# A message-passing network on one core: the edge weights leave the one-hot matrix, the features become three bf16 terms, and GpSimd multiplies

## The chip, the cores and the metric

The kernel runs on one core of a Trainium2 chip. Its time is device time in microseconds; the smaller is the better. TensorE is called PE, VectorE DVE, ScalarE ACT, GpSimd POOL and SyncE SP, as the profiles call them. PEld is PE's weight load.

## The reference

128 graphs of 64 nodes, 128 features a node, go through four layers, each a residual with a layer norm. The first two are continuous-filter layers on the dense matrix `adj` of distances; the last two are graph convolutions with a normalised adjacency. Cut to what the change touches:

```python
# layer 0 (20 Gaussians, cosine cutoff at 5)
y = x @ w_in2f
W = ssp(f_ij @ fw1 + fb1) @ fw2 + fb2          # a filter of 128 values for every pair (i, j)
W = W * rcut[..., None]
agg = jnp.einsum('bjf,bijf->bif', y, W)
x = _layernorm(x + ssp(agg @ ow1 + ob1) @ ow2 + ob2)

# layer 1 (64 Gaussians, the edge weight A is adj itself, and it enters twice)
Wf = Wf * Am
y = jnp.einsum('bjf,bijf->bif', rf, Wf * Am)

# layers 2 and 3: graph convolutions with d^-1/2 (A + I) d^-1/2
```

So each edge (i, j) takes the features of node j, times a filter that depends on its distance, times a weight (`rcut` in layer 0, the square of `adj` in layer 1), and sums over j.

## The kernel before

Only edges are computed. Two graphs (a pair) are worked on together, graph 0 on partitions 0 to 63 and graph 1 on 64 to 127 wherever a tile is laid out by node. A first part, `compact`, sorts each row's edges into fixed slots: nodes are ordered by degree, and each row of eight nodes gets a fixed number of slots (141 in layer 0, 162 in layer 1). Of each slot three numbers are written to DRAM: the distance `d`, the neighbour's index `j` (bf16), and the weight `w`. For 8 pairs (a set) this is one bundle; the compaction of sets 1 to 7 runs beside the main loop, seven steps (`run(early, 7)`) and one scatter step (`run(side, 1)`) per iteration. POOL issues its indirect scatters and packing copies.

The main loop has 2 x 64 pairs (64 of layer 0, then 64 of layer 1) and three chunks a pair, 384 chunks and as many iterations. A chunk is 2 x 376 slots in layer 0 and 2 x 432 in layer 1. Its steps:

- `loads(n)`: SP reads d, j and w of a pair from DRAM, the same row broadcast to many partitions; w goes to the 64 partitions of its graph.
- `gaussians`: ACT squares and exponentiates d, ahead of the pair.
- `filter_in` (px, L1466): PE's first filter layer; ACT turns it into h with Exp and Ln (L740, the line of the helper that records all ACT work).
- `one_hot` (hot, L1451): DVE makes the matrix that gathers, `(j == row) * w`, 128 partitions, fp32.
- `gather` (pg, L1492): two fp32 matmuls of 64 rows, features times that matrix; ACT copies the result to SBUF as `g`.
- `filter_out` (pw, L1479): PE's second filter layer, 128 rows, fp32.
- `message` (m, L1507): DVE, `(pw + b2) * g`, pw in PSUM and g in SBUF.
- `slot_sums` (agg, L1525): eight DVE reduces per pair, three per iteration.

Iteration i runs `filter_in` of chunk i, `gather` of chunk i-1, and `filter_out` and `message` of chunk i-2. Between these stand single steps of generators (queues `nodes`, `befores`, `convs`, `last`) that `slot` advances: `node_before` (features of the next group of four pairs: transpose xT, copy xt L1226, matmul y L1232), `node_after` (zero entries' share in layer 0, output layers, back permutation, layer norm L1200 to L1207), and `graph_convs` (layers 2 and 3 for a group). A step that ends with a matmul group is followed, at the next `slot`, by the step that reads it:

```python
        before, owing = owing, None
        held = run(queue, 1)
        if before is not None and before is not queue:
            run(before, 1)
```

All engines run their instructions in exactly this written order (`in_order` at the end makes it so), and the DMAs of SP stand in one queue. In the groups that matter four pairs make twelve chunks, and I write "a group" for that. `late_constants` makes the vectors dinv2 and dinv3 of the convolutions, with two powers on POOL (L1168, L1171), near pairs 52 to 56.

Of the kernel before, what the change touches and what calls it, by code (L numbers as in the profile page):

```python
# [11 lines left out]
F32 = mybir.dt.float32  # L12
# [565 lines left out]
def sparse_stack(ctx: ExitStack, tc: tile.TileContext, t: dict, out: bass.AP, flag):  # L578
# [9 lines left out]


    nc = tc.nc  # L590
    x, adj = t["x"], t["adj"]
# [172 lines left out]
    ident = const.tile([P, P], F32, name="ident")  # L764
    make_identity(nc, ident)
    ones = const.tile([3, P], BF16, name="ones")
    nc.vector.memset(ones, 1.0)
# [256 lines left out]
    def loads(n):  # L1024


        layer, p = divmod(n, NP)
        size = GSLOTS[layer]
        s, at = p // 8, (p % 8) * 2 * size
        assert (layer, s) in stored, "slots are read before they are written"  # L1030
        d = edge.tile([P, GSLOTS[1]], F32, tag="d", name=f"d_{n}", bufs=3)
        j = edge.tile([P, GSLOTS[1]], BF16, tag="j", name=f"j_{n}")
        w = edge.tile([P, GSLOTS[1]], F32, tag="w", name=f"w_{n}")

        def load(to, name, first, n):

            nc.sync.dma_start(to, dram_ap(slots[layer, name][s], first, [[0, to.shape[0]], [1, n]]))

        if layer == 0:
            third = 2 * size // 3  # L1040
            for q in range(3):
                load(d[32 * q : 32 * (q + 1), 0:third], "d", at + q * third, third)
            d = d[0:96, 0:third]
        for b in range(2):
            rows, first = slice(A * b, A * (b + 1)), at + b * size
            if layer == 1:
                load(d[rows, 0:size], "d", first, size)
            load(j[rows, 0:size], "j", first, size)
            load(w[rows, 0:size], "w", first, size)
        return d, j, w  # L1050

# [99 lines left out]
    def late_constants():  # L1151


        eye = const.tile([P, A], F32, name="eye")
        nc.vector.tensor_add(eye, ident[:, 0:A], ident[:, A : 2 * A])
        deg = const.tile([P, NP], F32, name="deg")
        for s in range(NS):
            part_ = a_all[:, part(s), 0:A]
            nc.vector.tensor_add(part_, part_, eye.unsqueeze(1).to_broadcast([P, 8, A]))
            nc.vector.tensor_reduce(deg[:, part(s)], part_, AX.X, ALU.add)  # L1160
            yield
        g["dinv2"] = const.tile([P, NP], F32, name="dinv2")
        g["dinv3"] = const.tile([P, NP], F32, name="dinv3")
        some = const.tile([P, NP], F32, name="some")

        nc.vector.tensor_scalar(some, deg, 0.0, None, ALU.is_gt)
        nc.vector.tensor_scalar(g["dinv2"], deg, TINY, None, ALU.max)
        nc.gpsimd.tensor_tensor(g["dinv2"], g["dinv2"], neg_half, ALU.pow)  # L1168
        nc.vector.tensor_mul(g["dinv2"], g["dinv2"], some)
        nc.vector.tensor_scalar(g["dinv3"], deg, GCN_EPS, None, ALU.add)  # L1170
        nc.gpsimd.tensor_tensor(g["dinv3"], g["dinv3"], neg_half, ALU.pow)  # L1171
        yield

# [15 lines left out]
    def once(name, n, q):  # L1189

        if n < GS and rings:
            return tiled(name, n, q)
        return node.tile([P, GS * P], F32, tag=name, name=f"{name}_{q}", bufs=1)[:, 0 : n * P]

# [20 lines left out]
    def node_before(layer, q):  # L1215
# [19 lines left out]
        yield True  # L1235
        y = node.tile([P, n, C], F32, tag=f"y{n}", name=f"ys_{name}", bufs={GS: 3, 2: 1, 1: 2}[n])
        act(y, ps, AF.Copy)
        feats[layer, q] = y
        yield

    zblk = const.tile([P, GS, P], F32, name="zblk")
    nc.gpsimd.memset(zblk, 0.0)

    def zero_share(q, agg):

        n = agg.shape[1]
        rows = zero_rows.pop(q)
        for b in range(2):
            at = slice(b * A, (b + 1) * A)
            nc.vector.tensor_scalar(zblk[at, :, at], rows[at], 0.0, None, ALU.is_equal)  # L1250
        yield
        _, ps = bank(f"zT_{q}", n)
        for s in range(n):
            nc.tensor.transpose(ps[:, s, :], zblk[:, s, :], ident)
        yield True
        zt = by_pair(once("zt", n, q))
        act(zt, ps, AF.Copy)
        yield
        _, ps = bank(f"zs_{q}", n)
        y = feats[0, q]  # L1260
        for s in range(n):
            nc.tensor.matmul(ps[:, s, :], lhsT=y[:, s, :], rhs=zt[:, s, :], start=True, stop=True)
        yield True
        nc.vector.scalar_tensor_tensor(agg, ps, zero_filter, agg, ALU.mult, ALU.add)
        yield

    def load_nodes(layer, q):
# [5 lines left out]
        if layer == 0:  # L1273
            rows = node.tile([P, GS, A], F32, tag="zr", name=f"zr_{q}")
            for s in range(GS):
# [170 lines left out]
    def one_hot(n):  # L1446

        _, j, wt = slot_data[n]
        size = GSLOTS[n // NP]
        hots[n] = edge.tile([P, GSLOTS[1]], F32, tag="hot", name=f"hot_{n}")  # L1450
        nc.vector.scalar_tensor_tensor(  # L1451
            hots[n][:, 0:size], j[:, 0:size], near, wt[:, 0:size], ALU.is_equal, ALU.mult
        )
# [30 lines left out]
    def gather(c):  # L1484
# [3 lines left out]
        at = slice(c["k"] * n, (c["k"] + 1) * n)  # L1488
        y = feats[c["at"]][:, c["s"], :]
        for b in range(2):  # L1490
            rows = slice(A * b, A * (b + 1))
            nc.tensor.matmul(  # L1492
                ps[:, b, 0:n], lhsT=y[rows, :], rhs=hots[c["n"]][rows, at],
                start=True, stop=True,
            )
        g_ = work.tile([P, 2, CHUNKS[1]], F32, tag="g", name=f"g_{c['id']}")
        c["g"] = g_[:, :, 0:n]
        act(c["g"], ps[:, :, 0:n], AF.Copy)

    def message(c):  # L1500
# [36 lines left out]
    last = []  # L1537
    slot_data, messages, aggs = {}, {}, {}

# [11 lines left out]
    for n in range(2):  # L1551
        slot_data[n] = loads(n)
    for s in (1, 2):
        load_set(s)
    run(deque([permuted(1), node_before(0, 0)]), -1)
    gaussians(0, 0)
    gaussians(0, 1)
    early = deque([gathering()])

# [21 lines left out]


    block = nc.cur_bb.bb.instructions
    before_loop = block[-1]
    past = [None] * 2
    for i in range(3 * N + 2):
        n, k = divmod(i, 3)
        c, c1, c2 = None, *past
        run(sums, 3)
        run(early, 7)  # L1590
        run(side, 1)
        if i == 3 * (NP + 1):
            assert not early and not side, "edges are still to be gathered"
            compacting.close()
# [7 lines left out]
        if n < N:  # L1602
# [6 lines left out]
            if k == 0:  # L1609
                if n + GS < N:  # L1610
                    ahead(n)
                if n + 2 < N:
                    slot_data[n + 2] = loads(n + 2)
                if c["s"] == min(2, len(range(NP)[GROUPS[layer][q]]) - 1):
                    load_nodes(layer, q)
                one_hot(n)
            filter_in(c)
        slot(nodes)
        if k < 2 and befores:
            slot(befores)  # L1620
# [7 lines left out]
        if k < 2 and n + 1 < N:  # L1628
            gaussians(n + 1, k)
        if c1 is not None:  # L1630
            gather(c1)
        slot(convs[1])
        for queue in last:
            slot(queue)
        past = [c, c1]
    run(sums, -1)
# [51 lines left out]
```

## Time and profile before

| | |
|---|---|
| median of 3 runs | 1931.93 us (1928.95 to 1933.0) |
| the profiled execution | 1935.16 us, span of its instructions 1933.4 us |
| mean granted TensorE clock | 0.950 |
| start, until the first chunk's Exp | 88.2 us |
| pairs 0 to 64 (layer 0) | 88.2 to 963.1 us |
| pairs 64 to 128 (layer 1) | 963.1 to 1855.7 us, last chunk's Exp |
| tail | 1855.7 to 1933.4 us |
| bytes moved by DMA | 214.96 MB, mean 111 GB/s |

The page gives busy time of each engine and its share of the span; a busy PE is not PE at its peak, since matmuls overlap. In a group's row the last part is: busy time of the group, mean duration of one instruction in ns, then idle time of the engine just before them and what ended it. An instruction's line is that of `kernel.py` before the change, and line numbers after it are larger by up to 25.

### The profile page before, as it was taken

The page shows a single profiled execution, that of the slowest core. Times are in us where ns is not written, and L with a number is a line of the kernel's source. Part 1 is how long each engine was busy: PE and PEld are TensorE (multiplying, and loading weights), DVE is VectorE, ACT ScalarE, POOL GpSimd, SP SyncE. Part 2 cuts the span into 40 slices and gives each one's busy share as a digit, 9 for nine tenths or more (in the row PEclk, how much of TensorE's full clock was granted, in tenths as well). Part 3 has the DMA queues.
Part 4 walks back from the last instruction along what each step waited for, and adds up shares of the span by engine and source line. Part 5 has one row for each costly group of instructions (what it writes and reads, how often), then busy time and mean ns, then how long its engine had stood idle before and what let it go on. Part 6 is the DMA issues. An engine that isn't in the chain of part 4 may idle for free.

```text
span 1933.4 us, 23695 instructions
## 1 busy us (share of the span) xinstructions
PE 1633.8 (85%) x6790; PEld 803.8 (42%) x6790; DVE 1587.6 (82%) x4298; ACT 1431.7 (74%) x1679; POOL 625.9 (32%) x920
## 2 busy tenths in 40 slices
PE   0288888788887999969988999999999999999975
PEld 0133343343333444424443544444454444444444
DVE  6579889888988777767778888888888888988984
ACT  1277767777766888848898978878888788888840
POOL 2423424342332232141112123323223333322435
PEclk9999898988998999979999999999999999999985
DMA  5355444363443444424566544645455455554400
GB/s 140 87 130 125 110 112 113 91 140 99 101 106 90 110 119 111 112 55 104 122 140 141 135 118 112 137 113 139 119 121 137 110 126 120 128 129 119 105 7 13
DMA packets 120595, 214.96 MB, mean 111 GB/s; under 512 B 41845, under 2 KB 68614, under 8 KB 120454
## 3 DMA queue, kind: packets, MB, share of 16 engines
q1 hardware_dynamic: 111776, 207.19, 44.4%
q0 software_dynamic: 4352, 5.02, 0.8%
q10 hardware_dynamic: 4326, 1.13, 0.3%
q8 instruction: 56, 0.92, 0.2%
q14 instruction: 85, 0.70, 0.1%
HBM read 200.92 MB, written 12.34 MB: 110 GB/s over the span
## 4 chain that ended last, share of the span: by engine, by line
PE 44%; DVE 33%; ACT 8%; issue 6%; POOL 3%; DMA 3%; SPq 1%; DVEq 0%; POOLq 0%; ACTq 0%
PE pw L1479 16%; DVE m L1507 9%; PE pg L1492 8%; DVE agg L1525 7%; PE px L1466 7%; DVE hot L1451 3%; ACT g L740 2%; PE y L1232 2%; ACT h L740 2%; ACT d L740 2%; PE back L1320 2%; DVE st L1200 2%; DVE mv L1201 2%; PE u L1291 1%; DVE at L961 1%
## 5 line engine op out<-in xcount | busy, mean ns | idle before, releaser
L740 ACT ACTIVATE g<-pg 128x752 f32<-128x752 f32 (+1 forms) x384 | 321.2, 836 | 255.8 <-PE pg L1492 249.2
L1525 DVE TENSOR_REDUCE agg<-m 128x16 f32<-128x336 f32 (+11 forms) x1024 | 417.1, 460 | 2.1
L740 ACT ACTIVATE h<-h,half 128x752 f32<-128x752 f32 (+2 forms) x385 | 372.4, 967 | 12.5
L1492 PE MATMUL pg<-hot,ys 64*128 64x376 f32 (+1 forms) x1536 | 374.3, 565 | 0.1
L1479 PE MATMUL pw<-h,w_L_gnn_fw 128*128 128x376 f32 x768 | 314.4, 536 | 35.8 <-DVE m L1507 35.7
L1507 DVE SCALAR_TENSOR_TENSOR m<-pw,c_L_gnn_b,g 128x432 f32<-128x432 f32 x384 | 245.1, 662 | 105.1 <-PE pw L1479 89.5
L1479 PE MATMUL pw<-h,w_L_gnn_W2T 128*128 128x432 f32 x768 | 321.2, 541 | 3.7 <-DVE m L1507 3.7
L1507 DVE SCALAR_TENSOR_TENSOR m<-pw,c_L_gnn_fb,g 128x376 f32<-128x376 f32 x384 | 219.7, 604 | 104.3 <-PE pw L1479 101.7
L1205 POOL TENSOR_TENSOR rs<-rs,neg_half 128x4 f32<-128x4 f32 (+2 forms) x70 | 68.6, 980 | 572.3 <-DVE rs L1203 570.4
L740 ACT ACTIVATE h<-px,c_L_gnn_b 128x864 f32<-128x864 f32 x192 | 187.4, 976 | 66.0 <-PE px L1466 66.0
L1479 PEld LDWEIGHTS pw<-h,w_L_gnn_fw 128*128 128x128 f32 x768 | 145.4, 209 | 150.6 <-DVE m L1507 66.0
L1492 PEld LDWEIGHTS pg<-hot,ys 64*128 64x128 f32 x1536 | 119.0, 190 | 202.1 <-ACT h L740 85.2
L1466 PE MATMUL px<-d,fw 32*128 32x376 f32 x768 | 180.4, 546 | 23.5 <-ACT h L740 21.1
L1479 PEld LDWEIGHTS pw<-h,w_L_gnn_W2T 128*128 128x128 f32 x768 | 131.9, 190 | 145.8 <-issue 90.4
L1451 DVE SCALAR_TENSOR_TENSOR hot<-j,row,w 128x1128 f32<-128x1128 bf16 (+1 forms) x128 | 191.3, 1495 | 0.0
L1466 PE MATMUL px<-d,w1t 64*128 64x432 f32 x768 | 178.4, 541 | 0.0
L740 ACT ACTIVATE h<-px,c_L_gnn_fb 128x752 f32<-128x752 f32 x192 | 169.6, 883 | 10.3 <-PE px L1466 6.2
L740 ACT ACTIVATE d<-d,neg_off 96x752 f32<-96x752 f32 (+1 forms) x128 | 145.0, 1133 | 0.0
L1466 PEld LDWEIGHTS px<-d,fw 32*128 32x128 f32 x768 | 59.7, 189 | 131.6 <-issue 66.0
L868 POOL DMA_INDIRECT rows<-comb,goes x64 | 70.6, 1103 | 121.9 <-DMA rows<-comb,goes 88.1
L1207 POOL TENSOR_SCALAR x_all<-ny,mv,rs 128x128 f32<-128x128 f32 x128 | 100.4, 795 | 3.6
L1466 PEld LDWEIGHTS px<-d,w1t 64*128 64x128 f32 x768 | 68.3, 186 | 56.2 <-issue 40.2
(210 smaller groups left out, 2078.6 us busy)
## 6 DMA issues: line engine op xcount, KB each, us to landing
d<-d_dram SPq DMA_DIRECT2D x128, 324.0 KB
w<-w_dram SPq DMA_DIRECT2D x128, 324.0 KB
w<-w_dram SPq DMA_DIRECT2D x128, 282.0 KB
j<-j_dram SPq DMA_DIRECT2D x128, 162.0 KB
j<-j_dram SPq DMA_DIRECT2D x128, 141.0 KB
d<-d_dram SPq DMA_DIRECT2D x192, 94.0 KB
x_all<-in_x_dram SPq DMA_DIRECT2D x8, 512.0 KB
cb<-code_dram SPq DMA_DIRECT2D x31, 128.0 KB
```

The costliest lines, as they stand in the source:

```text
L740: latest = nc.scalar.activation(out_, in_, func, **kw)
L868: nc.gpsimd.indirect_dma_start(out=into, out_offset=bass.IndirectOffsetOnAxis(ap=at, axis=0), in_=rows, in_offset=None,)
L1200: nc.vector.bn_stats(stats[:, s, :], y[:, s, :])
L1201: nc.vector.bn_aggr(mv[:, s, :], stats[:, s, :])
L1205: nc.gpsimd.tensor_tensor(rstd, rstd, neg_half[:, 0:n], ALU.pow)
L1207: nc.gpsimd.tensor_scalar(dst[:, s, :], y[:, s, :], mv[:, s, 0:1], rstd[:, s : s + 1], ALU.subtract, ALU.mult,)
L1451: nc.vector.scalar_tensor_tensor(hots[n][:, 0:size], j[:, 0:size], near, wt[:, 0:size], ALU.is_equal, ALU.mult)
L1466: nc.tensor.matmul(ps[:, b, 0:n], lhsT=w["w1"][rows, :], rhs=d[rows, col : col + n], start=True, stop=True,)
L1479: nc.tensor.matmul(ps[:, 0 : c["size"]], lhsT=c["w"]["w2"], rhs=c["h"][:, b, :], start=True, stop=True)
L1492: nc.tensor.matmul(ps[:, b, 0:n], lhsT=y[rows, :], rhs=hots[c["n"]][rows, at], start=True, stop=True,)
L1507: nc.vector.scalar_tensor_tensor(messages[n][:, b, at], c["pw"][b][:, 0:size], c["w"]["b2"], c["g"][:, b, :], ALU.add, ALU.mult,)
L1525: nc.vector.tensor_reduce(av[:, :, :, r], v[:, :, :, BASES[layer][r] : BASES[layer][r] + CAPS[layer][r]], AX.X, ALU.add,)
```

## The change

The one-hot matrix holds only zeros and ones, in bf16. The features are kept as three bf16 terms whose sum is the fp32 value, so that a gather is three bf16 products per graph, added up in PSUM. The weights are loaded on all 128 partitions, both graphs side by side, and POOL multiplies g by them in place after ACT's copy.

```diff
 node_before
-        y = node.tile([P, n, C], F32, tag=f"y{n}", ...)
-        act(y, ps, AF.Copy)
+        y = node.tile([P, 3, n, C], BF16, tag=f"y{n}", ...)
+        rest = by_pair(node.tile([P, 512], F32, tag="xt", ...)[:, 0 : n * P])
+        act(y[:, 0], ps, AF.Copy)
+        nc.vector.tensor_sub(rest, ps, y[:, 0])
+        nc.gpsimd.tensor_copy(y[:, 1], rest)
+        nc.gpsimd.tensor_tensor(y[:, 2], rest, y[:, 1], ALU.subtract)
 one_hot
-        hots[n] = edge.tile([P, GSLOTS[1]], F32, tag="hot", name=f"hot_{n}")
-        nc.vector.scalar_tensor_tensor(
-            hots[n][:, 0:size], j[:, 0:size], near, wt[:, 0:size], ALU.is_equal, ALU.mult
-        )
+        hots[n] = edge.tile([P, GSLOTS[1]], BF16, tag="hot", name=f"hot_{n}")
+        nc.vector.tensor_scalar(
+            hots[n][:, 0:size], slot_data[n][1][:, 0:size], near, None, ALU.is_equal
+        )
 gather
-        for b in range(2):
-            rows = slice(A * b, A * (b + 1))
-            nc.tensor.matmul(
-                ps[:, b, 0:n], lhsT=y[rows, :], rhs=hots[c["n"]][rows, at],
-                start=True, stop=True,
-            )
-        g_ = work.tile([P, 2, CHUNKS[1]], F32, tag="g", name=f"g_{c['id']}")
+        for i in range(3):
+            for b in range(2):
+                rows = slice(A * b, A * (b + 1))
+                nc.tensor.matmul(
+                    ps[:, b, 0:n], lhsT=y[rows, i, c["s"], :], rhs=hots[c["n"]][rows, at],
+                    start=i == 0, stop=i == 2,
+                )
+        g_ = work.tile([P, 2, CHUNKS[1]], F32, tag="g", name=f"g_{c['id']}", bufs=3)
         act(c["g"], ps[:, :, 0:n], AF.Copy)
+        nc.gpsimd.tensor_tensor(c["g"], c["g"], weights[c["n"]][:, :, at], ALU.mult)
 load_weights (new; the weights leave loads)
+        weights[n] = edge.tile([P, 2, GSLOTS[1]], F32, tag="w", name=f"w_{n}")
+        for b in range(2):
+            load_slots(weights[n][:, b, 0:size], "w", n, b * size)
```

The order changes with it. `gather` works on the chunk of its own iteration, no longer on the one before; `one_hot` of the next pair and `load_weights` two pairs ahead stand at the end of a pair's third iteration; a `befores` step runs in one iteration of three, no longer in two:

```diff
-        if k < 2 and befores:
+        if k == 1 and befores:
             slot(befores)
...
-        if c1 is not None:
-            gather(c1)
+        if c is not None:
+            gather(c)
+        if k == 2 and n + 1 < N:
+            one_hot(n + 1)
+        if k == 2 and n + 2 < N:
+            load_weights(n + 2)
...
-        if i == 3 * (NP + 1):
+        if i == 3 * (NP + 6):
             compacting.close()
```

In `late_constants` the two powers of 128x64 become sixteen of 128x8, seven early steps apart:

```diff
-        nc.gpsimd.tensor_tensor(g["dinv2"], g["dinv2"], neg_half, ALU.pow)
+        for i in (2, 3):
+            dinv = g[f"dinv{i}"]
+            for s in range(NS):
+                yield from (None for _ in range(7))
+                nc.gpsimd.tensor_tensor(dinv[:, part(s)], dinv[:, part(s)], neg_half[:, 0:8], ALU.pow)
```

The share of the zero entries in layer 0 (`zero_share`) goes the same way, a bf16 transpose and three bf16 products. Tiles `no` and `ny` share buffers with `na` and `nh`.

## The prediction

> **What bounds the kernel now.** I read the page first: who is busy, and the chain that ended last.
>
> ```profile
> PE 1633.8 (85%) x6790; PEld 803.8 (42%) x6790; DVE 1587.6 (82%) x4298; ACT 1431.7 (74%) x1679; POOL 625.9 (32%) x920
> PE 44%; DVE 33%; ACT 8%; issue 6%; POOL 3%; DMA 3%; SPq 1%; DVEq 0%; POOLq 0%; ACTq 0%
> PE pw L1479 16%; DVE m L1507 9%; PE pg L1492 8%; DVE agg L1525 7%; PE px L1466 7%; DVE hot L1451 3%; ACT g L740 2%; PE y L1232 2%; ACT h L740 2%; ACT d L740 2%; PE back L1320 2%; DVE st L1200 2%; DVE mv L1201 2%; PE u L1291 1%; DVE at L961 1%
> ```
>
> PE and DVE share the chain. The gather (pg, 8%) and the one-hot (hot, 3%) are what the change shrinks; POOL, where the new product goes, is two thirds idle. Next the windows, cut where the timeline shows the work to change: pairs 76 to 124 (steady layer 1), then pairs 40 to 52 and 52 to 56 of layer 0.
>
> ```profile
> 1114.00:1801.40 687.40, 644.54 (x2845) 326.33 (x2846) 600.34 (x1277) 571.28 (x627) 227.71 (x256) 1.00 0.52 124
> 655.00:798.50 143.50, 132.52 (x561) 62.52 (x560) 108.29 (x232) 119.23 (x152) 42.49 (x64) 0.98 0.45 115
> 798.50:868.00 69.50, 48.93 (x190) 22.89 (x190) 47.35 (x102) 40.22 (x51) 29.35 (x18) 0.83 0.30 74
> ```
>
> After length come PE, PEld, DVE, ACT and POOL busy, granted clock, DMA share, GB/s. I reckon per group: four pairs, twelve chunks. Steady layer 1 is 12 groups of 57.3 us: PE 53.7 busy, DVE 50.0, ACT 47.6, POOL 19.0. PE is within 3.6 us of the whole. The third row is one group that took 69.5 us where its neighbours take 47 to 48. The same query at every 100 us gives for 100 to 600 us (layer 0 beside compaction, groups of 57.7 us) DVE 88.3%, PE 84.0%, POOL 35.0%: there DVE is the fuller. Last, the groups by form, the waits, and single instructions in the timeline:
>
> ```profile
> L1492 PE MATMUL pg<-hot,ys 64*128 64x432 f32 x768 | 191.1, 575 | 0.1
> L1492 PE MATMUL pg<-hot,ys 64*128 64x376 f32 x768 | 183.1, 555 | 0.1
> L1451 DVE SCALAR_TENSOR_TENSOR hot<-j,row,w 128x1296 f32<-128x1296 bf16 x64 | 99.8, 1560 | 0.0
> L1451 DVE SCALAR_TENSOR_TENSOR hot<-j,row,w 128x1128 f32<-128x1128 bf16 x64 | 91.5, 1430 | 0.0
> ```
>
> ```profile
> PE y L1232 <- DVE xt L1226: 48.3, 21, 4.5
> ```
>
> ```profile
> 305.05 1.61 DVE L911 TENSOR_SCALAR w<-dc 128x141 f32<-128x141 f32 x1
> ...
> 486.44 2.17 DVE L1451 SCALAR_TENSOR_TENSOR hot<-j,row,w 128x1128 f32<-128x1128 bf16 x1
> ...
> 842.12 10.58 POOL L1168 TENSOR_TENSOR dinv<-dinv,neg_half 128x64 f32<-128x64 f32 x1 [34.38 <-DVE dinv L1167]
> ...
> 854.03 2.88 PE L1479 MATMUL pw<-h,w_L_gnn_fw 128*128 128x376 f32 x4 [12.11 <-DVE m L1507]
> ...
> 1232.61 1.27 POOL L1394 TENSOR_TENSOR x_all<-x_all,b_L_gnn_b 128x512 f32<-128x512 f32 x1
> ...
> 1748.31 0.73 POOL L1228 TENSOR_TENSOR x_all<-x_all,b_L_gnn_bd 128x256 f32<-128x256 f32 x1
> ```
>
> Three things to see. POOL's two-input product is straight in its size: 0.73 us for 256 elements, 1.27 for 512. One long POOL instruction (the power, 10.6 us, twice) stopped DVE and then PE for 12 us. And DVE and POOL block each other: the one-hot of 486.44 usually takes 1.38 us, but began under a POOL product (486.14 to 487.41) and took 2.17; POOL products that begin under a one-hot take 2.3 to 2.5 us instead of 1.27. The L911 row takes 0.24 us elsewhere and here waited behind four POOL instructions in a row.
>
> **The change, part by part.** *Gather.* A chunk's two fp32 products are issued as four matmuls (1536 in 384 chunks); busy time per chunk is 183.1/192 = 0.95 us (layer 0) and 191.1/192 = 1.00 (layer 1). K=128 of the same width takes 321.2/192 = 1.67 us, so the two 64-row halves overlap. No bf16 matmul of this shape is in the trace; the nearest (bias row, 3x512, L1422) is one instruction where fp32 needs two. I count an fp32 matmul as twice two passes: eight passes become six, at equal overlap three quarters: -0.24 and -0.25 us per chunk, about -94 us of PE in all. Bounds: perfect overlap of three pairs, a bf16 pass at half an fp32 instruction's serial share (1.67/8 = 0.21 us), 0.63 us per chunk (-143); per instruction, not per pass, 6 x 0.25 = 1.5 us (+190). I stay at three quarters because the time of px, 32 rows a tile, also goes by overlap, not count.
>
> *One-hot.* 128 times 1.43 or 1.56 us becomes a one-input compare, bf16 to bf16. Nearest: DVE's bf16 add, 682 ns for 1024 and 1213 for 2048, 0.52 ns an element plus 0.15 us: 0.73 and 0.82 us; not below half of that, not above today's. -92 us of DVE. [...]
>
> *Weights by POOL.* 192 products of 752 and 192 of 864 elements. From the two rows above, 2.1 ns an element plus 0.18 us: 1.78 and 2.02 us, 730 us on POOL. The third term and the copy (L1253 of the new file, a cast and a subtract of 512) are about 0.7 + 1.27 us per group; DVE gets one subtract of 512, 0.68 us. POOL per layer-1 group: 19.0 + 12 x 2.02 + 2.0 = 45.2 of 57.3. What hides it: the gather now runs an iteration earlier, so a product has more than one iteration (4.8 us) between ACT's copy and the message. Without that cover every chunk pays its 2 us. Queued behind a waiting product on POOL are the layer norms (4.2 us), conv scalings and scatters. They need at most 2 us of DVE's lead, so I cost no stall there.
>
> *The port.* This is the term without a price. A DVE operation that met a running POOL product waited out its rest less 0.15 to 0.2 us. Message and reduce, DVE's bulk, read one operand from SBUF and show no lengthening (604 against 604 ns under POOL work). Exposed per layer-1 group: four one-hots, a node add (L1307), two ELU adds (L1344), one compare (L1304), 8; in the compacting stretch about 15. POOL products run 40 to 45% of the time, mean rest 1 us: 0.35 us each from products, up to 0.55 with other POOL work in layer 1. Ends: 0, and 1.4 us (the L911 row less its usual 0.24). I take 0.55 x 8 = 4.5 and 0.35 x 15 = 5.2 us per group. [...]
>
> *Moved.* befores step at k = 1 only: PE's y matmuls come three iterations after the copy they waited for, 48.3/21 = 2.3 us each, mostly layer 0. The power becomes 16 short ones (rows of 1, 2, 4 columns: 0.57, 0.72, 1.03 us, so about 1.65 at 8), one per iteration. SP: the weights double (282 KB to 564, 324 to 648 KB, 256 times); in layer 1 +0.66 MB per 14.3 us on 124 GB/s lifts the share from 0.52 to about 0.71. SP now waits for POOL's last product of a pair before loading weights, and d and j of a later pair stand behind that; they have a pair's time, 14 us, and the present bursts last about 7 us, so nothing is charged. Later closing of the compaction pool, shared tags and bf16 zero share: under 3 us, nothing.
>
> **The sum.** Layer 1, 12 groups: PE 53.7 - 3.0 = 50.7; DVE 50.0 - 3.0 + 0.7 + 4.5 = 52.2; POOL 45.2. With the 3.6 us that lie beside the fullest engine now, 54.3 by PE, 55.8 by DVE; I take 55.5: -22 us. Compacting, 9 groups: DVE 50.9 - 2.8 + 0.7 + 5.2 = 54.0, but its 6.8 us idle shrinks by PE's 2.9 and the y wait's 2.3: about -0.5 each, -5. Pairs 40 to 52, three groups, DVE light: -3.5 each (the gather and half the y wait), -10. Group 52 to 56: 69.5 back to its neighbours' 48, less about 5 for a crowded POOL: -18. Pairs 56 to 76: five groups at -2.5, -12. Tail -2, first weights +3. Sum -66. The profiled execution took 1935.2 us (span 1933.4, 1.8 around it), so 1869; its median run is 1931.9, 3 us less: 1866.
>
> **The rivals.** *One, slower:* the port. If an exposed DVE operation waits 0.9 us (POOL fuller, its instructions back to back as before the L911 row), layer-1 DVE is 54.9 and the group about 58.3 (+12 us), the compacting group 62.3 busy and 64.5 long (+61), pairs 40 to 76 keep -5, the power -18: +50, about 1982. It decides from about 0.6 us a wait. For it: POOL goes from 35% to about 75% busy there. Against: waits outside products are rare. The variant with instructions priced alike in the gather ends there too. *Two, faster:* the compare is twice as fast, the port waits are under 0.2 us, PE sets the pace: layer 1 -36, compacting 9 x -5 = -45, the rest -50: 1801. For it: message and reduce never slowed. *Three, loads:* the wait on SP makes d late by half a microsecond per pair, 128 x 0.5 = +64: 1930, no change. That the change does not do what it says is not open: the new order holds 384 POOL products and six gather matmuls a chunk.
>
> **How the numbers follow.** Forecast (1830 to 1905) 0.45, rival two 0.22, rival three 0.10, rival one 0.23. Differences under 0.2% (4 us) cannot be told here. Rival three splits 0.04 faster, 0.04 same, 0.02 slower: faster 0.71, same 0.04, slower 0.25. The range 1790 to 1980 leaves out the far half of rival one and the tip of rival two.
>
> **What would show it.** Gather busy per chunk near 0.72 us; hot 0.5 to 0.85 us with some at 2; POOL product rows near 1.8 and 2.0 us; no 12 us PE gap; y waits gone; DVE m waiting for POOL g seldom. A large "DVE m <- POOL g" or hot rows of 2 us and more throughout prove rival one; ACT waiting for DMA d proves rival three.

## The result and the profile after

The changed kernel takes 2021.68 us (median, 2017.44 to 2026.69), the kernel before beside it 1932.47 us (1928.95 to 1934.61): a ratio of 1.0465, 95% interval 1.0436 to 1.0493. It is slower by 89 us where I forecast 66 us less. Its profiled execution took 2017.44 us, with a span of 2015.6.

The page of the changed kernel, busy time and the chain that ended last:

```profile
PE 1612.4 (80%) x7622; PEld 786.2 (39%) x7622; DVE 1649.2 (82%) x4333; ACT 1433.5 (71%) x1679; POOL 1386.3 (69%) x1386
DVE 27%; PE 24%; POOL 20%; issue 11%; DMA 10%; ACT 5%; SPq 1%; POOLq 0%; DVEq 0%; ACTq 0%
PE pw L1498 10%; POOL g L1519 8%; DVE m L1528 6%; DVE agg L1546 6%; DMA d<-d_dram 4%; DMA rows<-comb,goes 4%; POOL x_all L1219 3%; PE px L1485 3%; PE pg L1512 3%; DVE hot L1470 3%; POOL perm L871 2%; ACT g L741 2%; POOL rows L871 2%; DVE er L1364 2%; PE u L1311 1%
```

Of the four compute engines only POOL is fuller than before by share (32% to 69%), and it is still not full; PE and ACT fell, DVE stayed at 82%. What the chain shows is hand-over: POOL went from 3% to 20%, DMA from 3 to 10, PE from 44 to 24. Time is lost between engines, not on one of them. The windows of steady layer 1 (pairs 76 to 124, 12 groups of four pairs), of the compacting stretch (pairs 4 to 40, 9 groups) and of the group 52 to 56:

```profile
1143.80:1875.90 732.10, 643.27 (x3130) 328.82 (x3130) 637.74 (x1291) 571.28 (x625) 524.62 (x424) 0.96 0.57 160
139.00:687.70 548.70, 422.73 (x1927) 190.96 (x1928) 459.15 (x1624) 381.94 (x471) 383.92 (x488) 0.85 0.48 141
838.70:897.30 58.60, 49.22 (x217) 22.50 (x218) 47.03 (x102) 40.22 (x51) 35.82 (x35) 0.80 0.41 127
```

A layer-1 group takes 61.0 us (57.3 before), a compacting group 61.0 (57.7). In layer 1 PE is busy 53.6 us per group, as before (53.7), though its gather became lighter; DVE has 53.1, POOL 43.7. The fullest engine now leaves 7.4 us of a group idle, where it left 3.6. The clock in layer 1 fell from 1.00 to 0.96. Group 52 to 56, where the long powers stood, came down from 69.5 to 58.6.

The groups of instructions, by form:

```profile
L1519 POOL TENSOR_TENSOR g<-g,w 128x864 f32<-128x864 f32 x192 | 390.7, 2039 | 195.8 <-ACT g L741 175.0 <-issue 19.4 <-POOL blocks L1380 0.7
L1519 POOL TENSOR_TENSOR g<-g,w 128x752 f32<-128x752 f32 x192 | 343.0, 1789 | 156.6 <-ACT g L741 153.1 <-DMA zr<-perm 1.7
L1512 PE MATMUL pg<-hot,ys 64*128 64x376 bf16 x1152 | 139.5, 352 | 6.9 <-DVE hot L1470 6.4 <-ACT g L741 0.5
L1512 PE MATMUL pg<-hot,ys 64*128 64x432 bf16 x1152 | 139.1, 347 | 14.3 <-ACT g L741 9.8 <-DVE hot L1470 4.4
L1470 DVE TENSOR_SCALAR hot<-j,row 128x1296 bf16<-128x1296 bf16 x64 | 67.4, 1053 | 0.0
L1364 DVE SCALAR_TENSOR_TENSOR er<-em,er 128x512 f32<-128x512 f32 x30 | 52.6, 1755 | 0.0
L1215 DVE TENSOR_SCALAR rs<-mv 128x4 f32<-128x4 f32 x61 | 24.8, 407 | 2.1
```

The gather has 278.6 us, 95.6 less. The one-hot of 1296 columns takes 0.54 us when nothing hinders it (its lowest records), but 1.05 on average. The ELU add (er) took 681 ns before and takes 1755; the layer norm's add of four columns (rs) went from 169 to 407, and single ones to 1.85 us. The waits:

```profile
PEld pw L1498 <- DVE m L1528: 156.9, 194, 6.8
DVE m L1528 <- POOL g L1519: 71.5, 45, 6.8
ACT d L741 <- DMA d<-d_dram: 48.8, 27, 4.6
```

PE's weight loads wait twice as long for the message as before (156.9 us for 80.3), the message waits for the product, and ACT waits for distances, which it did not before. One case from the timeline of the changed kernel (start, length):

```profile
1407.70 1.25 PE L1498 MATMUL pw<-h,w_L_gnn_W2T 128*128 128x432 f32 x3
...
1412.06 2.01 POOL L1519 TENSOR_TENSOR g<-g,w 128x864 f32<-128x864 f32 x1 [2.40 <-ACT g L741]
1412.24 1.85 DVE L1215 TENSOR_SCALAR rs<-mv 128x4 f32<-128x4 f32 x1
...
1414.01 0.72 DVE L1546 TENSOR_REDUCE agg<-m 128x16 f32<-128x256 f32 x2
...
1414.78 1.13 PE L1311 MATMUL u<-agg,w_L_gnn_Wd1T 128*128 128x512 f32 x2 [3.16 <-DVE agg L1546]
...
1417.03 2.90 PE L1498 MATMUL pw<-h,w_L_gnn_W2T 128*128 128x432 f32 x4
```

An operation of 512 numbers begins 0.18 us behind a product and ends only with it; the reduces stand behind it on DVE; PE waits 3.16 us for them, some 1.7 of it the add's lengthening; and the matmuls after that take 0.73 us each where three took 0.42 each ten microseconds earlier. The granted clock is 1.00 from 1400 to 1414.8 us, 0.82 from there to 1417, 0.56 to 1420 and 1.00 to 1425. So here a stall cost PE twice: its 3.16 us, and slower matmuls after it.

### The profile page after: what moved, and what is told of

It reads as the page before. It is cut to its first block, busy times and chain, and to the rows that moved or that the text cites. A ratio compares the mean times of both kernels' runs of the same rounds, so it can differ in the third digit from the quotient of the medians.

```text
span 2015.6 us, 25949 instructions
## 1 busy us (share of the span) xinstructions
PE 1612.4 (80%) x7622; PEld 786.2 (39%) x7622; DVE 1649.2 (82%) x4333; ACT 1433.5 (71%) x1679; POOL 1386.3 (69%) x1386
## 4 chain that ended last, share of the span: by engine, by line
DVE 27%; PE 24%; POOL 20%; issue 11%; DMA 10%; ACT 5%; SPq 1%; POOLq 0%; DVEq 0%; ACTq 0%
PE pw L1498 10%; POOL g L1519 8%; DVE m L1528 6%; DVE agg L1546 6%; DMA d<-d_dram 4%; DMA rows<-comb,goes 4%; POOL x_all L1219 3%; PE px L1485 3%; PE pg L1512 3%; DVE hot L1470 3%; POOL perm L871 2%; ACT g L741 2%; POOL rows L871 2%; DVE er L1364 2%; PE u L1311 1%
## 5 line engine op out<-in xcount | busy, mean ns | idle before, releaser
L1519 POOL TENSOR_TENSOR g<-g,w 128x752 f32<-128x752 f32 (+1 forms) x384 | 733.7, 1914 | 352.4 <-ACT g L741 328.1
L1498 PE MATMUL pw<-h,w_L_gnn_fw 128*128 128x376 f32 x768 | 337.5, 569 | 76.0 <-DVE m L1528 75.1
L1498 PE MATMUL pw<-h,w_L_gnn_W2T 128*128 128x432 f32 x768 | 340.8, 568 | 7.5 <-DVE m L1528 7.5
L1512 PE MATMUL pg<-hot,ys 64*128 64x376 bf16 (+1 forms) x2304 | 278.6, 350 | 21.2 <-DVE hot L1470 10.8
L1498 PEld LDWEIGHTS pw<-h,w_L_gnn_fw 128*128 128x128 f32 x768 | 151.1, 217 | 206.2 <-DVE m L1528 127.2
L1485 PE MATMUL px<-d,fw 32*128 32x376 f32 x768 | 190.3, 574 | 37.7 <-ACT h L741 35.0
L1498 PEld LDWEIGHTS pw<-h,w_L_gnn_W2T 128*128 128x128 f32 x768 | 138.3, 200 | 158.7 <-issue 76.3
L1512 PEld LDWEIGHTS <-ys 64*128 64x128 bf16 x2304 | 85.1, 96 | 265.8 <-issue 175.4
L741 ACT ACTIVATE d<-d,neg_off 96x752 f32<-96x752 f32 (+1 forms) x128 | 145.7, 1138 | 51.4 <-DMA d<-d_dram 48.8
L1470 DVE TENSOR_SCALAR hot<-j,row 128x1128 bf16<-128x1128 bf16 (+1 forms) x128 | 119.3, 932 | 0.0
L871 POOL DMA_INDIRECT perm<-a_all,index x64 | 63.9, 999 | 50.9 <-DVE index L811 35.2
```

Of the source, the lines that this page charges most:

```text
L741: latest = nc.scalar.activation(out_, in_, func, **kw)
L871: nc.gpsimd.indirect_dma_start(out=into, out_offset=bass.IndirectOffsetOnAxis(ap=at, axis=0), in_=rows, in_offset=None,)
L1470: nc.vector.tensor_scalar(hots[n][:, 0:size], slot_data[n][1][:, 0:size], near, None, ALU.is_equal)
L1485: nc.tensor.matmul(ps[:, b, 0:n], lhsT=w["w1"][rows, :], rhs=d[rows, col : col + n], start=True, stop=True,)
L1498: nc.tensor.matmul(ps[:, 0 : c["size"]], lhsT=c["w"]["w2"], rhs=c["h"][:, b, :], start=True, stop=True)
L1512: nc.tensor.matmul(ps[:, b, 0:n], lhsT=y[rows, i, c["s"], :], rhs=hots[c["n"]][rows, at], start=i == 0, stop=i == 2,)
```

## The experiments

Theory at the outset: the port, as I call it when a DVE operation lasts longer beside a POOL instruction (the rs add above: 1.85 us for 0.17). The product lengthens one-hots, adds and compares on DVE, and that is all the loss. Rivals: the message waits for a product that POOL's queue delays; the doubled loads of weights, and SyncE's wait for POOL before them, come late; POOL's own other work stands behind the products; the new order is itself bad. In runs 1 to 6 and 9 to 12 the features are not weighted, so the output is not the reference's.

One number is worked out for each run from its trace, "lengthening": for every form of DVE instruction, the time above that form's third-percentile duration, where it is more than 60 ns, summed. It is 11.0 us before and 178.2 after; of the 178.2 the one-hots have about 52 us, er 32, the compares bk (L1324) and zblk (L1267) 26 and 22, the node add nh (L1327) 15 and rs 15.

**1. A power in the product's place.** Ten columns of a power last about as long as a product (1914 ns in the mean of both sizes).

```diff
-        nc.gpsimd.tensor_tensor(c["g"], c["g"], weights[c["n"]][:, :, at], ALU.mult)
+        lo = c["k"] * n
+        nc.gpsimd.tensor_tensor(
+            c["g"][:, 0, 0:10], weights[c["n"]][:, 0, lo : lo + 10], pos_one, ALU.pow
+        )
```

> In the place of each product POOL takes a power of ten columns of the weights and writes it into g: about 2 us on POOL (rows: 1.69 us at 8 columns, 1.03 at 4), the same place in POOL's queue, the same wait of the message for POOL and of SP for the weights' buffer. What it leaves out is the product, so g is not weighted. It differs from the change in what POOL reads and writes while it runs: ten columns, not 864. If DVE's waits behind POOL's products are the cause (port), one-hot rows fall to 0.5 us, the 178 us by which DVE's rows are lengthened nearly vanish, and the time falls to 1880 or less. If the wait of the message in POOL's queue (queue), the loads (loads) or the new order (order) are the cause, it stays at 2000 or more.

Measured 1943.99 us, 1.0024 (1.0007 to 1.0041; a ratio to the kernel before, with its interval, here and below), between the two expectations. The step took 1986 ns and lengthening fell to 5.9 us, yet only 78 us came back. The port is not the whole. The chain of this kernel, then its message row for layer 0:

```profile
POOL 31%; PE 26%; DMA 11%; DVE 10%; issue 10%; ACT 8%; SPq 1%; POOLq 0%; ACTq 0%; DVEq 0%
L1533 DVE SCALAR_TENSOR_TENSOR m<-pw,c_L_gnn_fb,g 128x376 f32<-128x376 f32 x384 | 217.4, 603 | 123.6 <-POOL g L1522 78.7 <-PE pw L1500 44.2
```

POOL leads the chain, and the message's wait for it grew. What one wait gave up, the next took.

**2. The product aside.** It is written over the weights, which nobody reads after it, so the message need not wait.

```diff
-        nc.gpsimd.tensor_tensor(c["g"], c["g"], weights[c["n"]][:, :, at], ALU.mult)
+        wt = weights[c["n"]][:, :, at]
+        nc.gpsimd.tensor_tensor(wt, c["g"], wt, ALU.mult)
```

> POOL makes the same product of the same size, but writes it over the weights, and the message reads g without it: the weighting is left out of the result. The product still runs beside DVE, still follows ACT's copy and still holds the weights' buffer; only the message no longer waits for it. Port, loads or order: 1990 or more (at most the 72 us of DVE m waiting for POOL g are touched, and most of that comes back elsewhere). Queue: 1900 or less.

2008.39 us, 1.0354 (1.0332 to 1.0376): 13 us less; lengthening stays at 160.0.

**3. No loads of weights** (the product's second factor is resident).

```diff
-        for b in range(2):
-            load_slots(weights[n][:, b, 0:size], "w", n, b * size)
+        pass
...
+        nc.gpsimd.tensor_tensor(c["g"], c["g"], resident[:, :, 0:n], ALU.mult)
```

> The weights are not loaded; POOL multiplies g by a resident tile of ones, so the weighting is left out. 155 MB of DMA and SP's wait for POOL go. Loads: ACT's 49 us of waiting for d go and with what hangs on them the time falls to 1940 or less. Port, queue or order: 1995 to 2020.

1973.75 us, 1.0194 (1.0169 to 1.0218), between the two expectations: 48 us less, and ACT's wait for distances is gone. Most of it (3.0 us in each of 9 groups, 17 us in pairs 40 to 52) is in layer 0.

**4. No product,** loads kept: the line of the product is left out.

> POOL's product is left out, so g is not weighted; the weights are still loaded, twice as many bytes, and the order is the new one. Port and queue alike: 1860 or less, since POOL goes back to a third busy and the gather's 95 us and the one-hot's 120 us stay saved. Loads or order: 1980 or more.

1763.28 us, 0.9096 (0.908 to 0.9112). The windows of layer 1 and of the compacting stretch:

```profile
1013.60:1635.40 621.80, 603.84 (x3130) 311.81 (x3130) 559.95 (x1287) 565.78 (x625) 238.40 (x279) 1.00 0.65 188
132.90:602.60 469.70, 391.94 (x1927) 180.09 (x1928) 417.50 (x1634) 379.89 (x473) 188.61 (x384) 0.91 0.59 168
```

51.8 and 52.2 us per group. So everything that is lost, and more, comes with the product: 258 us. The same 3130 layer-1 matmuls have 603.8 us here and 643.3 with the product; these 39.4 us are a third of the 110.3 us that layer 1 differs by, and go with the clock, 1.00 against 0.96.

**5. The power aside:** neither port nor message wait, and POOL does not wait for ACT's copy either, since this power does not touch g.

```diff
+        lo = c["k"] * n
+        wt = weights[c["n"]][:, 0, lo : lo + 10]
+        nc.gpsimd.tensor_tensor(wt, wt, pos_one, ALU.pow)
```

> The weights are not multiplied in: in each chunk a power of ten columns by one, about 2.0 us on POOL as the product was, is taken in the tile of the weights itself, so that neither does it lengthen VectorE's steps (the power in the product's place left 5.9 us of lengthening) nor does the message wait for it. POOL's queue stays as full and the weights' loads as large. Together with the product (2021.7), the power in its place (1944.0), the product aside (2008.4) and no product (1763.3) this fills a square of port held or not, message waiting or not. Theory 'late message': what the power in the product's place still lost, 181 us, was the message waiting behind POOL's queue; then about 1790 (1765 to 1820). Rival 'full queue': the wait only took the place of others; POOL's other work (scatters, packs, layer norms, the sums with the bias) and SyncE's loads, that wait for the weights' readers, are late all the same; then 1900 to 1940, and little is left of waits of the message for POOL. A time of about 1850 would be some of each.

1843.76 us, 0.9547 (0.9528 to 0.9565): between the two theories. POOL is as busy as in the changed kernel (1404.6 us for 1386.3). Three groups, to be read against those of the changed kernel:

```profile
L1472 DVE TENSOR_SCALAR hot<-j,row 128x1296 bf16<-128x1296 bf16 x64 | 36.8, 575 | 0.0
L1366 DVE SCALAR_TENSOR_TENSOR er<-em,er 128x512 f32<-128x512 f32 x30 | 20.5, 683 | 0.0
L1217 DVE TENSOR_SCALAR rs<-mv 128x4 f32<-128x4 f32 x61 | 10.6, 174 | 2.1
```

The copy is a further difference between this run and runs 1 and 2. In those, as in the changed kernel, POOL's step stands behind ACT's copy of g, and whatever follows it on POOL stands behind the copy too. The layer-1 windows of runs 1, 2 and 5, then POOL's wait for the copy in runs 1 and 2, and the row of run 5, whose powers are kept waiting for 8.5 us in all:

```profile
1131.70:1807.50 675.80, 625.01 (x3130) 317.61 (x3130) 561.73 (x1289) 566.87 (x626) 513.27 (x424) 0.98 0.64 173
1147.20:1873.20 726.00, 647.71 (x3130) 329.41 (x3131) 623.86 (x1291) 569.38 (x625) 528.52 (x424) 0.95 0.59 161
1064.90:1711.80 646.90, 611.25 (x3130) 314.55 (x3131) 564.21 (x1292) 566.17 (x625) 514.37 (x424) 0.99 0.67 181
POOL g L1522 <- ACT g L741: 278.1, 127, 7.6
POOL w L1520 <- ACT g L741: 316.7, 136, 7.4
L1523 POOL TENSOR_TENSOR w<-w,pos_one 128x10 f32<-128x10 f32 x384 | 761.4, 1997 | 8.5 <-DMA w<-w_dram 3.3 <-issue 1.9
```

A layer-1 group takes 56.3, 60.5 and 53.9 us. In runs 1 and 2 PE's weight loads for the convolutions' `gx` wait 27.4 and 30.9 us for POOL's layer norms, in the changed kernel 27.8, here 1.1. So what this run saves over run 1 (100 us) and over run 2 (165) is not the message's wait or the port alone. No run has POOL's wait for the copy by itself.

**6. Loads unread.** The product is g times g, so that SyncE waits for nobody.

```diff
+        nc.gpsimd.tensor_tensor(c["g"], c["g"], c["g"], ALU.mult)
```

> The weights are loaded as before but nothing reads them: the product is the gathered features by themselves, of the same size and shape. POOL and the port are as in the changed kernel, the bytes are too; only SyncE no longer waits for POOL before it loads the weights of the next pair but one, nor do the loads of offsets and distances behind them. Taking the loads away as well gave 1973.8, 48 us less than the changed kernel's 2021.7. Theory 'SyncE held': the 48 us come from loads that start late behind that wait: 1970 to 1985, ACT's waits for distances fall from 48.8 us to under 10. Rival 'bytes': the doubled weight loads themselves delay the scatters' and rows' transfers: 2010 to 2025.

1911.77 us, 0.9877 (0.9841 to 0.9913): under both expectations, because the product had become shorter (1548 ns in the mean for 1914) and lengthening fell to 129.6. Two things had changed; the run does not tell the theories apart.

**7. The order alone.** Arithmetic of before, order of the changed kernel; only the loads of weights stand where they stood before, in a pair's first iteration.

```diff
-        nc.gpsimd.tensor_tensor(c["g"], c["g"], weights[c["n"]][:, :, at], ALU.mult)
...
+        nc.vector.scalar_tensor_tensor(
+            hots[n][:, 0:size], slot_data[n][1][:, 0:size], near, weights[n][:, 0:size],
+            ALU.is_equal, ALU.mult,
+        )
```

> The arithmetic of the kernel before (features in float32, a weighted one-hot by VectorE, no product) in the order of the changed kernel: gather in its chunk's own iteration, next pair's one-hot ahead, node work only in the middle iteration, powers split, three buffers for the gathered features. The kernel without the product was at 1763.3, 170 us under the kernel before (1935). Theory 'both count': gather and one-hot save 94 us of TensorE and 92 us of VectorE, which are filled in turn, and the order saves the rest, some 50 to 80 us: 1860 to 1890. Rival 'order': the order alone brings most of it, the lighter gather and one-hot little, since the chain of nodes ends last: 1780 to 1830. Rival 'no order': the order brings nothing by itself: 1925 to 1940.

1841.99 us, 0.9539 (0.9519 to 0.9559): under the first theory's 1860. It beats both kernels and leaves out nothing of the computation. Windows (layer 1, compacting stretch) and chain:

```profile
1042.20:1705.60 663.40, 644.01 (x2842) 326.39 (x2843) 598.22 (x1274) 570.33 (x626) 223.98 (x254) 1.00 0.53 128
130.30:616.50 486.20, 412.73 (x1675) 190.90 (x1675) 445.26 (x1623) 382.31 (x471) 180.12 (x366) 0.94 0.46 117
PE 47%; DVE 32%; ACT 7%; issue 5%; POOL 4%; DMA 2%; SPq 1%; DVEq 0%; POOLq 0%; ACTq 0%
```

In layer 1 PE is as busy as before (53.7 us a group), and only the idle time beside it shrank, from 3.6 to 1.6 us.

**8. The weights put into the one-hot by POOL,** once in a pair, with the gather of before.

```diff
+        hot = edge.tile([P, GSLOTS[1]], BF16, tag="is", name=f"is_{n}")[:, 0:size]
+        nc.vector.tensor_scalar(hot, slot_data[n][1][:, 0:size], near, None, ALU.is_equal)
+        hots[n] = edge.tile([P, GSLOTS[1]], F32, tag="hot", name=f"hot_{n}")
+        nc.gpsimd.tensor_tensor(hots[n][:, 0:size], hot, weights[n][:, 0:size], ALU.mult)
...
-        if k == 2 and n + 1 < N:
+        if k == 0 and n + 1 < N:
             one_hot(n + 1)
```

> As the kernel with the order alone, but VectorE makes the plain bf16 one-hot (0.5 us) a pair ahead and POOL multiplies the weights into it once in a pair, 128x1128 in float32 (about 2.6 us by the product's 1.79 us for 752 elements), in place of three products of 2.0 us; the gather stays at 8 passes. POOL gets some 320 us in place of 734 and holds the port less than half as long, and nobody waits for it within three chunks. Theory 'full queue' (cost in step with POOL's time): the product's 258 us for 734 us of POOL make 112 us here, against 92 us less on VectorE: no better than the order alone, within 25 us of it. Rival 'late message and port': with the lead of a whole pair and a third of the port the cost is under 40 us, so 30 to 60 us under the order alone.

1863.66 us, 0.9651 (0.9634 to 0.9668): 22 us over the order alone, with 320.5 us of POOL and 47.1 of lengthening. The longest of the waits on POOL:

```profile
POOL hot L1465 <- PE pg L1504: 216.9, 35, 13.0
```

It is a wait for a free buffer, up to 13.0 us, and the layer norms stand behind it. The number fits "full queue"; the trace points to this wait rather than POOL's fullness, since the loss is in layer 1 (a group of 57.7 us, the order alone 55.3), where POOL is over half idle, and not in the compacting stretch (53.5 for 54.0). That is argued: a third buffer was not tried.

**9 to 11. Loads unread again, and POOL's time by itself.** A resident factor, broadcast; the same on half the chunk; and a power on a tile of its own.

```diff
+        one = resident[:, 0:1].unsqueeze(2).to_broadcast([P, 2, n])
+        nc.gpsimd.tensor_tensor(c["g"], c["g"], one, ALU.mult)
...
+        one = resident[:, 0:1].to_broadcast([P, n])
+        nc.gpsimd.tensor_tensor(c["g"][:, 0, :], c["g"][:, 0, :], one, ALU.mult)
...
+        nc.gpsimd.tensor_tensor(junk, junk, pos_one, ALU.pow)
```

> The weights are loaded as before but nothing reads them: the product's second factor is a resident one, broadcast, so that the product has its size and should keep its 1.9 to 2.0 us (the features by themselves took only 1.55 us and so made the run before this one two changes at once). Theory 'SyncE held': the 48 us that no loads of weights gave against the changed kernel (1973.8 for 2021.7) come from loads that start late behind SyncE's wait for POOL: 1970 to 1985, nearly all in the stretch of the compaction. Rival 'bytes': 2010 to 2025. The features by themselves gave 59.4 us per group of four pairs there, for 58.0 without the loads and 61.0 in the changed kernel, with a shorter product, which speaks for the bytes at least in part; I expect 1985 to 2015.

1911.08 us, 0.9902 (0.9875 to 0.993): the broadcast factor too made the product short, 1547 ns. A miss for the same reason as run 6.

> The same with the product over one of the two halves of the chunk alone (376 columns in place of 752, about 1.0 us): the other half is not multiplied. POOL gets some 375 us in place of 735. With no product 1763.3, the features by themselves (593 us of POOL) 1911.8 and the full one this gives a curve of time over POOL's time. Theory 'in step' (each us that POOL multiplies costs the same 0.25 to 0.35 us): 1855 to 1895. Rival 'fullness' (POOL's gaps take the first half, the cost comes with the last of it): 1780 to 1830.

1805.98 us, 0.9348 (0.9323 to 0.9374), inside "fullness": the first 335 us of POOL cost 43 us, the next 259 (run 9) cost 105. POOL's 335.0 us in pieces of 0.87 us lengthened DVE by 34.6 us in all; the 593.5 us of run 9, in pieces of 1.55, by 133.2. The shorter step was met less often, and each meeting cost less: 80 lengthened instructions by 0.43 us in the mean, against 172 by 0.77.

> The weights are loaded but not read, and in the product's place stands a power of ten columns of a tile of its own, 2.0 us on POOL: nobody waits for it, it waits for nothing, it does not hold the port (13.0 us of lengthening in the run with the power over the weights), and SyncE does not wait for POOL. What is left against no product (1763.3) is only POOL's own other work standing behind it. The power over the weights was at 1843.8. Theory 'SyncE held': the 80 us between those two are loads that start late behind POOL's readers: 1765 to 1790. Rival 'full queue': they are scatters, packs, layer norms and sums behind 2 us steps: 1820 to 1845.

1799.64 us, 0.9313 (0.9287 to 0.9339): of the 80 us between no product and the power aside, about half each: neither theory alone. The windows (layer 1, compacting stretch):

```profile
1049.40:1671.20 621.80, 603.86 (x3130) 311.83 (x3131) 559.71 (x1287) 565.52 (x626) 513.88 (x422) 1.00 0.66 187
134.80:636.60 501.80, 394.47 (x1927) 181.80 (x1928) 415.29 (x1630) 380.51 (x471) 408.96 (x494) 0.88 0.53 157
```

Layer 1 has the 621.8 us of the kernel without a product, to the tenth, with POOL busy 514 us of them. There POOL's time by itself cost nothing. In the compacting stretch it cost 3.6 us a group: packs, and with them probably scatters, stand behind the powers (DVE waits 41.0 us for POOL's packs, 12.9 without a product).

**12. Two streams, loads unread:** a resident row of a quarter, read again for each quarter.

```diff
+        v = c["g"].rearrange("p b (r k) -> p b r k", r=4)
+        one = resident[:, 0 : n // 4].unsqueeze(1).unsqueeze(1).to_broadcast([P, 2, 4, n // 4])
+        nc.gpsimd.tensor_tensor(v, v, one, ALU.mult)
```

> As the run with the resident one broadcast, which kept the loads of weights unread but whose product took only 1.55 us; here the second factor is a resident row of ones of a quarter of the chunk's length, read again for each quarter, so that POOL has two streams to read and the product should take the 1.92 us that it took with a resident factor of full size. The weights are loaded and not read; they are not multiplied in. It stands between the changed kernel (2021.7, loads that wait for POOL) and the kernel without the loads (1973.8), with the same product. Theory 'SyncE held': the 48 us between those come from loads that wait for POOL: 1965 to 1985, and a group of four pairs in the compaction takes 58 us. Rival 'bytes': 2005 to 2022 and 60 to 61 us. If the product takes 1.55 us again, about 1911 as in the run before.

1984.89 us, 1.0213 (1.0186 to 1.0239), at the edge of "SyncE held".

```profile
L1523 POOL TENSOR_TENSOR g<-g,resident 128x864 f32<-128x864 f32 x192 | 391.4, 2044 | 163.7 <-ACT g L741 163.0
L1523 POOL TENSOR_TENSOR g<-g,resident 128x752 f32<-128x752 f32 x192 | 317.5, 1656 | 166.0 <-ACT g L741 155.6 <-DMA d<-d_dram 8.4
```

In layer 1 the product has its full length (2044 ns), in layer 0 only 1656. ACT's wait for distances fell to 1.2 us with all bytes still loaded: that wait is SyncE's. By the medians 37 of the 48 us of the loads are SyncE's wait for POOL, the shorter layer-0 product among them, and 11 the bytes. The bytes are not shown, though: the ratios, 1.0213 here and 1.0194 without loads, have intervals that overlap. A compacting group took 60.2 us here, 2.2 more than without loads, but the profiled executions are the slowest of this kernel (1991.96 us) and the fastest of that one (1965.42).

| kernel | us | compacting group | layer-1 group | lengthening |
|---|---|---|---|---|
| before | 1932 | 57.7 | 57.3 | 11 |
| order alone | 1842 | 54.0 | 55.3 | 9 |
| no product | 1763 | 52.2 | 51.8 | 12 |
| power on its own tile | 1800 | 55.8 | 51.8 | 11 |
| power aside | 1844 | 56.2 | 53.9 | 13 |
| power in its place | 1944 | 60.5 | 56.3 | 6 |
| product aside | 2008 | 60.7 | 60.5 | 160 |
| changed kernel | 2022 | 61.0 | 61.0 | 178 |

(Groups are from the profiled executions. The kernel before, measured beside each of them, was at 1931.7 to 1940.6 us, so a few us between rows mean nothing.)

Read downwards from "no product", leaving out "product aside": POOL's time 36 us; SyncE's wait for POOL 44; the message's wait together with POOL's wait for the copy 100; the port 78; 258 in all. By ratios to before these are 42, 45, 92 and 85. By the other way, over "product aside", the port together with POOL's wait for the copy costs 165 and the message's wait then 13. The two ways agree if POOL's wait for the copy alone is worth some 87 us and the rest adds up; they agree as well if port and message wait stand in for each other. The runs do not tell these apart. By ratios to before, the order brings 4.6%, the light gather and one-hot 4.4%, and the product takes 13.7%.

## Why the prediction was wrong

The forecast was -66 us and the change made +89. Three terms of the sum failed: what POOL's lateness costs ("I cost no stall there") and what the loads cost ("nothing is charged") were put at nothing, and the port was put into DVE's busy time, where most of it vanished beside PE.

*Gather, product.* Right: 0.73 us a chunk and -95.6 us of PE for -94; 1.789 and 2.039 us for 1.78 and 2.02; POOL 43.7 us per layer-1 group for 45.2. The passes of an fp32 matmul were my count, shown by no row of before; an fp32 gather instruction of 432 columns had 0.249 us of busy time before (191.1/768), a bf16 one 0.121 after (139.1/1152).

*One-hot.* Unhindered 0.50 and 0.54 us for my 0.73 and 0.82. The row I took, a bf16 add of 682 ns for 1024 elements, was the nearest, and too dear.

*The port.* The size was right in the compacting stretch, 48.7 us in 9 groups or 5.4 for 5.2. In layer 1 it was 78.1 in 12, 6.5 for 4.5, with 0.7 of it the rs add, that I had not counted. DVE's filling came out as worked: 53.1 us a group for 52.2. What failed is the step after it.

*The sum.* "With the 3.6 us that lie beside the fullest engine now" is the step that failed for the port. I put the port into DVE's busy time, found PE nearly level, and let the idle time stand, so that 4.5 us of port cost the group 1.2 (55.5 for the 54.3 by PE). But a lengthened add is a wait for whoever comes next: PE for the reduces behind it, then PE at a lower clock (0.56 in the case shown). In layer 1 the port's 6.3 us of lengthening per group cost 4.7 us of span (changed kernel less power in its place, two steps of like length). From the power aside to the product aside 5.0 us of lengthening came with 6.6 of span, POOL's wait for the copy included. The 3.6 us were no constant either: the order alone brought them to 1.6.

*The cover.* "I cost no stall there" failed too, on both sides of the product. One iteration between copy and message covers a product of 2 us, not one that stands behind layer norms of 3.1 us, scatters and earlier products on POOL: where the message waited for it in the changed kernel (45 times), the product began 4.9 us after its copy in the mean. And what is queued behind a waiting product came late: PE's `gx` loads waited 27.8 us for layer norms. With the port out of the way the two together cost 100 us, 4.3 per compacting group and 2.4 per layer-1 group. How the 100 divide stays open. In the compacting stretch a group takes 60.5 us or more with either the port or the message's wait; POOL waits for the copy in both.

*Loads.* "Nothing is charged": up to 48 us; from the power on its own tile to the power aside, SyncE's wait for POOL cost 44. Rival three had named its sign, ACT waiting for distances, and 48.8 us of that came; but it is the smaller part of the loss.

*Moved.* I credited the order with the y wait and the powers, in layer 0, and with nothing in layer 1. Alone it brings 90, 24 of them in layer 1 (12 x 2.0). Which of its moves does this was not taken apart.

*Rivals.* One had the right sign and, in layer 1, its condition: without the rs adds 5.8/8 = 0.72 us a wait, above the 0.6 that decides. In the compacting stretch the wait stayed at 0.36, and there the loss came with the message's and POOL's waits and the loads instead. So 2022 lies beyond its 1982.

*Slips in the sum.* The compacting group's own terms (54.0 + 6.8 - 2.9 - 2.3 = 55.6) make -2.1 us a group and not -0.5, the group of the long powers by its terms -16.5 and not -18, 0.55 x 8 is 4.4, and the gather's lower bound comes to -136 and not -143. The first would have moved the forecast some 14 us further from the result; the others do not count.

## What to carry to other kernels

A step given to an idle engine is priced by what it delays, not by that engine's busy share: here 734 us on a POOL that was two thirds idle cost 258. Count who stands behind it in the same queue, what comes late while it waits for its own input, who waits for its result with how much lead, who now waits to load, and which DVE operations last longer beside it (here one-hots, compares and adds); charge most of each such wait (here 4.7 of 6.3 us) when the other engines are within a few us of full. And when a change carries an order with it, measure the order alone: here it was the part worth keeping, 1842 us.

## What the hardware showed that I had not expected

- A POOL power of 2 us, read from and written to SBUF, lengthened hardly any DVE instruction: beside 761 us of powers in the tile of the weights DVE's lengthening was 13.0 us, with no product 12.0, with products of 0.87 us 34.6 (335 us of POOL). Beside a product an add of 0.17 us took 1.85; beside the powers er took 683 ns and rs 174 in the mean, for 681 and 169 in the kernel before. There too a node add (nh, L1307) that began 3.5 us into a power of 10.72 us took 0.68 us, its usual time.
- A product with a broadcast factor, or of g with itself, was quicker: 1646 ns for 864 elements by broadcast, against 2039 with a second operand of full size, and 1547 and 1548 ns in the mean of both sizes against 1914. A factor of a quarter's length, read again, was not at 864 elements (2044), but was at 752 (1656 for 1789).
- DVE's message and reduces, one operand in SBUF, did not slow: the layer-1 message took 661 ns in the changed kernel and 662 without a product, and no message or reduce is among the lengthened instructions.
- After the idle stretch of 3.16 us shown above PE's matmuls ran slower, at a granted clock of 0.56. In the layer-1 windows PE sat idle for over 2.5 us at a time 11 times in the changed kernel and never in the kernel before, with a granted clock of 0.96 for 1.00; in the compacting stretch 19 times for 13, with 0.85 for 0.90.
